# A two-layer selective scan: from states x channels on the partitions to directions x images x states

## The chip, the core and the metric

The kernel runs on one core of a Trainium2 chip. Its time is the device time of one execution in microseconds. The core has TensorE (PE), VectorE (DVE), ScalarE (ACT), GpSimd (POOL) and SyncE (SP), which here only issues DMAs; 16 DMA engines move data between DRAM and the on-chip memory SBUF. TensorE writes to PSUM, which GpSimd can't read.

## The reference

The input is 4 images of 64 x 64 pixels and 96 channels. Two layers of the same kind (L0, L1) are followed by two token layers (L2, L3; linear attention and a quantised feed-forward net). The change touches L0 and L1. Each of them computes, per image:

```
xn = group norm of x;  xx, z = in_proj(xn)          # 192 channels each
xc = silu(conv3x3_depthwise(xx) + b)
for k in 4 directions (rows, columns, both reversed), L = 4096 steps:
    dts, B, C = x_proj[k](xc in order k)              # 6, 16, 16
    delta = softplus(dt_proj[k](dts) + bias)          # 192 channels
    h[e, n] = exp(delta[e] * A[e, n]) * h[e, n] + delta[e] * u[e] * B[n]
    y_k[e]  = sum over 16 states n of h[e, n] * C[n]
y = y_0 + y_1 + y_2 + y_3 (put back in pixel order) + D * u
x = x + out_proj(layernorm(y) * silu(z))
```

The recurrence over 4096 steps runs for 2 layers x 4 images x 4 directions x 192 channels x 16 states. All of it is in 32-bit floats.

## The kernel before

Everything is written with tiles; a scheduler puts the instructions of each engine in order by the program's order and by what is ready, and sets the waits. Each engine then runs its instructions in that order.

`ssm_layer` does one layer, image by image: `conv(b)`, the scans, `finish(b)`. The convolution and the input projection are one set of nine matmuls per 512 pixels (L194). The 4096 steps are cut into 8 chunks of 512. A step of the loop is one direction k and one chunk c, 32 an image. For each, `chunk_inputs` makes B and C by matmuls whose weights repeat each state's row 8 times (L214), so that the partitions hold 16 states x 8 channels; delta by matmuls (L229) and a softplus from six instructions (L237 to L248); and du = delta * u (L253), which goes to a scratch in DRAM (L256).

The 192 channels make 6 groups of 32 per step, and each group 4 tiles of 128 partitions (16 states x 8 channels) x 512 steps. `load` (L274) reads du back with every row repeated 16 times, 1 MB a group. Per tile `scan` repeats delta over the states by a matmul from 32 partitions (L285, into PSUM), takes the exponential (L291), multiplies du by B on DVE (L293) and scans on DVE (L297, `tensor_tensor_scan`). `weigh` copies the carry (L304) and multiplies by C on POOL (L306). `sum` adds the 16 states with a matmul to 32 columns (L313), and `keep` adds the result to `y` (L337). The stages of a group are issued one to three groups behind its scan, and pieces of the next step's `chunk_inputs` after each group. The convolution and `finish` (z, layernorm, output projection; L352 to L385) stand alone before and after an image's scans.

A load's access pattern in DRAM is, with counts outermost first, 16 (states, step 0), 8 (channels), 2048 contiguous values; in SBUF it is 128 partitions of 2048 values.

Of the kernel before, what the change touches and what calls it, by code (L numbers as in the profile page):

```python
# [9 lines left out]
F32 = mybir.dt.float32  # L10
# [4 lines left out]
AX = mybir.AxisListType  # L15
# [3 lines left out]
B = 4  # L19
HW = 64  # L20
L = HW * HW
# [4 lines left out]
K = 4  # L26
PAD = HW + 2
# [3 lines left out]
EG = 8  # L31
NT = 4
NB = 3
NJ = NT * NB
P = 128
# [4 lines left out]
SQRT_HALF = 0.7071067811865476  # L40

# [15 lines left out]

def rows(t):

    if len(t.shape) == 2:  # L60
        return t.rearrange("p (r w) -> p r w", w=HW)
    return t.rearrange("p h (r w) -> p h r w", w=HW)


class Consts:
    def __init__(self, nc, pool, a):
        def load(name, shape):
            t = pool.tile(shape, F32, name=name)
            nc.sync.dma_start(t, a[name])
            return t  # L70

        self.rep = load("rep", [P, NB, 128])
        self.sel = load("sel", [128, NB, 32])
        self.group = load("group", [C, C])
        self.mask = load("mask", [C, C])
        self.mean_e = load("mean_e", [P, P])
        self.mean_c = pool.tile([C, C], F32, name="mean_c")
        nc.vector.memset(self.mean_c, 1.0 / C)
        self.eps = pool.tile([128, 1], F32, name="eps")
        nc.vector.memset(self.eps, EPS)  # L80
        self.one = pool.tile([128, 1], F32, name="one")
        nc.vector.memset(self.one, 1.0)


def neg_rsqrt(nc, cst, var, ln, r, sq, n=C):

    nc.scalar.activation(ln, var, AF.Ln, bias=cst.eps[:n])
# [6 lines left out]
@with_exitstack  # L94
def ssm_layer(ctx: ExitStack, tc, cst, a, pre, x_in, x_out):

    nc = tc.nc
    wp = ctx.enter_context(tc.tile_pool(name=pre + "w", bufs=1))
    big = ctx.enter_context(tc.tile_pool(name=pre + "big", bufs=1))
    cp = ctx.enter_context(tc.tile_pool(name=pre + "chunk", bufs=1))  # L100
    sp = ctx.enter_context(tc.tile_pool(name=pre + "scan", bufs=6))
    small = ctx.enter_context(tc.tile_pool(name=pre + "small", bufs=2))
    dp = ctx.enter_context(tc.tile_pool(name=pre + "dram", bufs=3, space=DRAM))
    p_da = ctx.enter_context(tc.tile_pool(name=pre + "p_da", bufs=4, space=PSUM))
    p_y = ctx.enter_context(tc.tile_pool(name=pre + "p_y", bufs=1, space=PSUM))
    p_b = ctx.enter_context(tc.tile_pool(name=pre + "p_b", bufs=2, space=PSUM))
    p_one = ctx.enter_context(tc.tile_pool(name=pre + "p_one", bufs=1, space=PSUM))


    in_w = wp.tile([C, 4 * P], F32, name="in_w")  # L110
    nc.sync.dma_start(in_w, a[pre + "in_proj_w"])
    taps = wp.tile([C, 9, 2 * P], F32, name="taps")
    nc.sync.dma_start(taps, a[pre + "conv_w"].unsqueeze(0).broadcast_to([C, 9, 2 * P]))

    def small_w(name, shape):
        t = wp.tile(shape, F32, name=name)
        nc.sync.dma_start(t, a[pre + name])
        return t

    conv_b = small_w("conv_b", [P, 2])  # L120
    dt_b = small_w("dt_projs_bias", [P, K, 2])
    ds_k = small_w("Ds", [P, 2, K])
    gam = small_w("gamma", [P, 2])
    bet = small_w("beta", [P, 2])
    out_w = small_w("out_proj_w", [P, 2, C])
    a_col = small_w("A_logs", [128, K, 2, NJ])
    xp_t = small_w("x_proj_t", [P, K, 2, R + 2 * NS])
    xp_dt = small_w("x_proj_dt", [R, K, 2 * P])
    dt_w = small_w("dt_projs_weight", [R, K, 2 * P])


    nc.vector.tensor_tensor(
        taps, taps, in_w[:, : 2 * P].unsqueeze(1).broadcast_to([C, 9, 2 * P]), ALU.mult
    )

    nc.scalar.activation(a_col, a_col, AF.Exp)
    nc.vector.tensor_scalar_mul(a_col, a_col, -1.0)
    ds = wp.tile([P, 2], F32, name="ds")
    nc.vector.tensor_reduce(ds, ds_k, AX.X, ALU.add)

    bc_w = wp.tile([P, K, 2, 2, 128], F32, name="bc_w")
    dl_w = wp.tile([P, K, 2, 2 * P], F32, name="dl_w")
    for k in range(K):
        for h in range(2):
            nc.vector.tensor_copy(
                bc_w[:, k, h].rearrange("p m (n e) -> p (m n) e", e=EG),
                xp_t[:, k, h, R:].unsqueeze(2).broadcast_to([P, 2 * NS, EG]),
            )
            ps = p_one.tile([128, TC], F32, name="ps1")
            nc.tensor.matmul(  # L150
                ps[:, : 2 * P], xp_dt[:, k, h * P : (h + 1) * P], dt_w[:, k, :], start=True, stop=True
            )
            nc.scalar.copy(dl_w[:, k, h], ps[:, : 2 * P])

    stats_of = {}

    def conv(b):

        xn = big.tile([C, PAD, PAD], F32, name="xn")
        nc.gpsimd.memset(xn[:, 0, :], 0.0)  # L160
        nc.gpsimd.memset(xn[:, PAD - 1, :], 0.0)
        nc.gpsimd.memset(xn[:, 1 : PAD - 1, 0], 0.0)
        nc.gpsimd.memset(xn[:, 1 : PAD - 1, PAD - 1], 0.0)
        st = small.tile([C, NC, 6], F32, name="st")
        for c in range(NC):
            mid = xn[:, 1 + ROWS * c : 1 + ROWS * (c + 1), 1 : 1 + HW]
            nc.sync.dma_start(mid, rows(x_in[b, :, c * TC : (c + 1) * TC]))
            nc.vector.bn_stats(st[:, c, :], mid)  # L168
        mv = small.tile([C, 2], F32, name="mv")
        nc.vector.bn_aggr(mv, st.rearrange("p c s -> p (c s)"))  # L170

        ps = p_one.tile([128, TC], F32, name="ps1")
        nc.tensor.matmul(ps[:C, :1], cst.group, mv[:, 0:1], start=True, stop=True)
        gs = small.tile([C, 2], F32, name="gs", bufs=3)
        nc.vector.tensor_copy(gs[:, 0:1], ps[:C, :1])
        d = small.tile([C, 1], F32, name="d")
        nc.vector.tensor_tensor(d, mv[:, 0:1], gs[:, 0:1], ALU.subtract)
        nc.vector.scalar_tensor_tensor(d, d, d, mv[:, 1:2], ALU.mult, ALU.add)
        ps = p_one.tile([128, TC], F32, name="ps1")
        nc.tensor.matmul(ps[:C, :1], cst.group, d, start=True, stop=True)  # L180
        ln = small.tile([C, 2], F32, name="ln")
        neg_rsqrt(nc, cst, ps[:C, :1], ln[:, 0:1], gs[:, 1:2], ln[:, 1:2])
        nc.vector.tensor_scalar_mul(gs[:, 1:2], gs[:, 1:2], -1.0)
        stats_of[b] = gs
        for c in range(NC):
            mid = xn[:, 1 + ROWS * c : 1 + ROWS * (c + 1), 1 : 1 + HW]
            nc.vector.tensor_scalar(mid, mid, gs[:, 0:1], gs[:, 1:2], ALU.subtract, ALU.mult)
        xc = big.tile([P, 2, L], F32, name="xc")
        for c in range(NC):
            for h in range(2):  # L190
                ps = p_one.tile([128, TC], F32, name="ps1")
                for tap in range(9):
                    dy, dx = divmod(tap, 3)
                    nc.tensor.matmul(  # L194
                        rows(ps),
                        taps[:, tap, h * P : (h + 1) * P],
                        xn[:, ROWS * c + dy : ROWS * (c + 1) + dy, dx : dx + HW],
                        start=tap == 0,
                        stop=tap == 8,
                    )  # L200
                nc.scalar.activation(  # L201
                    xc[:, h, c * TC : (c + 1) * TC], ps, AF.Silu, bias=conv_b[:, h : h + 1]
                )
        return xc

    def chunk_inputs(xc, k, c, got):


        u = scan_view(xc, k, c)
        got["b"] = p_b.tile([128, TC], F32, name="b_ps")  # L210
        c_ps = p_one.tile([128, TC], F32, name="ps1")
        for m, ps in enumerate((got["b"], c_ps)):
            for h in range(2):
                nc.tensor.matmul(rows(ps), bc_w[:, k, h, m], u[:, h], start=h == 0, stop=h == 1)  # L214
        yield
        got["c"] = cp.tile([128, TC], F32, name="cc", bufs=2)
        nc.scalar.copy(got["c"], c_ps)  # L217
        yield
# [3 lines left out]
        top = cp.tile([P, 2, TC], F32, name="t0")  # L222
        e = cp.tile([P, 2, TC], F32, name="t1")
        ln = cp.tile([P, 2, TC], F32, name="t2")
        w = cp.tile([P, 2, TC], F32, name="t3")
        for m in range(2):
            raw = p_one.tile([128, TC], F32, name="ps1")
            for h in range(2):
                nc.tensor.matmul(  # L229
                    rows(raw),  # L230
# [29 lines left out]
    class Group:  # L260

        def __init__(self, k, c, h, i, got, carry, xc, y):
# [390 lines left out]
```

## Time and profile before

| | |
|---|---|
| median of 3 runs | 17764.24 us (17760.72 to 17765.47) |
| profiled execution | 17765.74 us, of which 17763.9 us are the span |
| mean granted TensorE clock | 0.716 |
| matmuls, vector, scalar, GpSimd instructions | 34144, 15421, 12017, 6700 |
| DMA, main queue | 1765.94 MB, 353160 packets |
| one image's scans, from 195 to 1830 us | DVE 1518.68 us busy, PE 1437.60, POOL 1079.63, ACT 757.18 |

The span is the time between the first and the last instruction. A group's row in the profile has the line, the engine, output and inputs with their shapes, the count, the busy time of the group in us, the mean duration of one in ns, and the idle time of the engine before them with what ended it. Where several run at once, busy time is less than count times mean. A 32-bit matmul appears as two records, one for each of its two passes.

### The profile page before, as it was taken

What the parts mean: (1) busy time and instruction counts of PE and PEld (TensorE: products, weight loads), DVE (VectorE), ACT (ScalarE), POOL (GpSimd) and SP (SyncE); (2) the same over time, 40 slices, a digit from 0 to 9 for tenths busy, and PEclk for the clock granted to TensorE, in tenths of its full rate; (3) what the DMA queues carried; (4) which work ended last, traced back from release to release, by engine and by line L of the source; (5) the groups of instructions that cost most, each with busy time, mean ns of one, the idle gap of its engine ahead of it and who ended that gap; (6) DMA issues with size and microseconds to landing.
All of it is one profiled execution on the core that took longest, in us unless ns stands there. A gap on an engine that the chain in (4) does not pass through costs nothing.

```text
span 17763.9 us, 120237 instructions
## 1 busy us (share of the span) xinstructions
PE 14593.3 (82%) x34144; PEld 4171.9 (23%) x34144; DVE 13631.7 (77%) x15421; ACT 7698.0 (43%) x12017; POOL 8983.9 (51%) x6700
## 2 busy tenths in 40 slices
PE   8888788887888788887888788887888788885555
PEld 2222222222222222222222222222222222222222
DVE  5999399975999489984999579993999669993333
ACT  3444344443444344442444344442444334444555
POOL 3666166653666266652666356661666346660000
PEclk8767777667767777677776777677767777676665
DMA  4555165543555155542555255552555345550000
GB/s 88 129 128 128 40 133 129 128 98 74 129 128 129 41 126 129 128 106 62 133 124 131 60 109 127 130 122 48 131 128 129 71 96 128 129 126 23 7 7 7
DMA packets 360991, 1786.21 MB, mean 101 GB/s; under 512 B 93550, under 2 KB 94960, under 8 KB 162760
## 3 DMA queue, kind: packets, MB, share of 16 engines
q1 hardware_dynamic: 353160, 1765.94, 44.8%
q10 hardware_dynamic: 7168, 12.59, 0.2%
q8 instruction: 275, 4.51, 0.1%
q14 instruction: 388, 3.18, 0.1%
HBM read 1658.82 MB, written 119.54 MB: 100 GB/s over the span
## 4 chain that ended last, share of the span: by engine, by line
PE 41%; POOL 18%; DVE 17%; issue 15%; ACT 9%; DMA 0%; DVEq 0%; POOLq 0%; SPq 0%; ACTq 0%
POOL st L306 13%; PE da L285 11%; DVE st L297 9%; PE y_ps L313 8%; PE ps L194 6%; PE b_ps L214 5%; PE ps L229 4%; DVE st L293 3%; POOL delta L248 3%; POOL t L246 3%; ACT L88 1%; ACT da L291 1%; PE ps L362 1%; PE ps L370 1%; PE y_ps L383 1%
## 5 line engine op out<-in xcount | busy, mean ns | idle before, releaser
L306 POOL TENSOR_TENSOR st<-st,cc 128x512 f32<-128x512 f32 x6144 | 7785.6, 1298 | 4253.5 <-ACT carry L304 2489.1
L297 DVE TENSOR_TENSOR_SCAN st<-da,carry,st 128x512 f32<-128x512 f32 x5376 | 6460.2, 1264 | 662.8 <-ACT da L291 661.6
L285 PE MATMUL da<-delta,rep 32*128 32x512 f32 x12288 | 5498.9, 884 | 812.6 <-DVE st L297 723.7
L291 ACT ACTIVATE da<-da,A_logs 128x512 f32<-128x512 f32 x6144 | 3907.5, 664 | 4885.7 <-PE da L285 4876.1
L313 PE MATMUL y_ps<-st,sel 128*32 128x512 f32 x12288 | 3321.2, 913 | 798.5 <-POOL st L306 626.8
L293 DVE TENSOR_TENSOR st<-st,b_ps 128x512 f32<-128x512 f32 x6144 | 3788.2, 678 | 0.0
L285 PEld LDWEIGHTS da<-delta,rep 32*128 32x128 f32 x12288 | 1744.2, 245 | 4783.9 <-DVE st L297 3466.9
L229 PE MATMUL ps<-xc,dl_w 128*128 128x512 f32 x2048 | 1445.5, 834 | 23.5 <-ACT cc L217 12.6
L313 PEld LDWEIGHTS y_ps<-st,sel 128*32 128x32 f32 x12288 | 486.1, 137 | 3388.2 <-POOL st L306 1708.4
L246 POOL TENSOR_TENSOR t<-t,t 128x1024 f32<-128x1024 f32 x256 | 603.3, 2357 | 1047.5 <-DVE t L244 1047.5
L194 PE MATMUL ps<-xn,taps 96*128 96x512 f32 x2304 | 1047.4, 609 | 93.2 <-ACT xc L201 68.4
L214 PE MATMUL b_ps<-xc,bc_w 128*128 128x512 f32 x1024 | 980.8, 1052 | 73.5 <-DVE st L293 73.5
L253 DVE TENSOR_TENSOR du<-delta,xc 128x512 f32<-128x512 f32 x512 | 870.3, 1739 | 178.3 <-POOL delta L248 177.7
L237 ACT ACTIVATE t<-ps,dt_projs_bias 128x512 f32<-128x512 f32 x512 | 351.7, 687 | 1373.1 <-PE ps L229 1324.1
L297 DVE TENSOR_TENSOR_SCAN st<-da,st 128x512 f32<-128x512 f32 x768 | 876.2, 1201 | 50.5 <-ACT da L291 49.9
L214 PE MATMUL ps<-xc,bc_w 128*128 128x512 f32 x1024 | 874.4, 987 | 27.9 <-ACT t L238 21.7
L160 POOL MEMSET xn<- 96x66 f32 x8 | 1.2, 150 | 1762.7 <-PE ps L194 1598.0
L168 DVE BATCH_NORM_STATS2 st<-xn 96x6 f32<-96x512 f32 x64 | 44.2, 690 | 871.9 <-DMA xn<-x 437.2
L244 DVE SCALAR_TENSOR_TENSOR t<-t,t 128x1024 f32<-128x1024 f32 x256 | 329.3, 1286 | 426.0 <-ACT t L242 426.0
L484 POOL MEMSET tn<- 1x4096 f32 x8 | 28.0, 3506 | 1194.7 <-PE pa L525 1027.6
L229 PEld LDWEIGHTS ps<-xc,dl_w 128*128 128x128 f32 x2048 | 398.0, 205 | 949.8 <-issue 600.4
L248 POOL TENSOR_TENSOR delta<-t,t 128x1024 f32<-128x1024 f32 x256 | 600.7, 2347 | 3.1
(118 smaller groups left out, 8712.8 us busy)
## 6 DMA issues: line engine op xcount, KB each, us to landing
st<-scratch SPq DMA_DIRECT2D x1536, 1024.0 KB
scratch<-du SPq DMA_DIRECT2D x1024, 96.0 KB
xr<-in_x SPq DMA_DIRECT2D x64, 192.0 KB
x<-xr ACTq DMA_DIRECT2D x64, 192.0 KB
xr<-x SPq DMA_DIRECT2D x64, 192.0 KB
xn<-in_x SPq DMA_DIRECT2D x32, 192.0 KB
xn<-x SPq DMA_DIRECT2D x32, 192.0 KB
t<-x SPq DMA_DIRECT2D x4, 1536.0 KB
```

The lines of the kernel that those rows point to most:

```text
L194: nc.tensor.matmul(rows(ps), taps[:, tap, h * P : (h + 1) * P], xn[:, ROWS * c + dy : ROWS * (c + 1) + dy, dx : dx + HW], start=tap == 0, ...
L214: nc.tensor.matmul(rows(ps), bc_w[:, k, h, m], u[:, h], start=h == 0, stop=h == 1)
L229: nc.tensor.matmul(rows(raw), dl_w[:, k, h, m * P : (m + 1) * P], u[:, h], start=h == 0, stop=h == 1,)
L246: nc.gpsimd.tensor_tensor(ln, ln, w, ALU.subtract)
L248: nc.gpsimd.tensor_tensor(delta, top, ln, ALU.add)
L253: nc.vector.tensor_tensor(rows(du[:, h]), rows(delta[:, h]), u[:, h], ALU.mult)
L285: nc.tensor.matmul(da, cst.rep[part, i], self.got["delta"][part, h], start=True, stop=True)
L291: nc.scalar.activation(da, da, AF.Exp, scale=a_col[:, k, h, j : j + 1])
L293: nc.vector.tensor_tensor(st[:, t], st[:, t], self.got["b"], ALU.mult)
L297: nc.vector.tensor_tensor_scan(st[:, t], da, st[:, t], 0.0 if c == 0 else col, ALU.mult, ALU.add)
L306: nc.gpsimd.tensor_tensor(st[:, t], st[:, t], self.got["c"], ALU.mult)
L313: nc.tensor.matmul(y_of[h][32 * t : 32 * t + 32], cst.sel[:, i], self.st[:, t], start=i == 0, stop=i == NB - 1,)
```

## The change

Two images are processed together as a phase; there are four phases (two layers, two pairs). The partitions of a scan tile hold 8 (direction, image) pairs x 16 states, a tile is one channel x 512 steps, and a unit is 24 channels of one chunk: 256 units of 12 slots with two tiles each.

- `prepare` makes, for a whole phase, the convolution and then for each image, chunk and direction B, C, delta and du, and stores them in DRAM; softplus is one ACT function. It is written as a generator.
- `load` fetches du for a unit in six DMAs of 1 MB (four channels each), each row repeated over 16 partitions, and delta in twelve small ones. `times_b` multiplies du by B on POOL, 128 x 2048 at a time.
- `scan` is as before but for the matmul, which repeats delta from 8 partitions.
- `weights` builds per chunk, on POOL, matrices with C times a mask of the eight pairs. `contract` multiplies by C and sums over the states in one matmul per four time steps: 16 matmuls a call, to four column groups, moving operand 96 columns whose innermost step is 512 values. ACT copies the result and 16 DMAs a unit store it in DRAM in an order that keeps (pair, time).
- `finish` reads y from DRAM, adds the directions with permutation matmuls, and does layernorm with pixels on the partitions. It is a generator too.
- `run` issues scans slot by slot; after each slot 1.5 pieces of `finish` of the phase before and then of `prepare` of the next phase. The first `prepare` and the last `finish` stand alone. Pixels are stored in another order, so that the token layers' load is strided.

```diff
-    class Group:
...
+    def steps(self, ph, sp, xc, xp, dt_w, i, k, c):
...
+        for h in range(2):
+            nc.tensor.matmul(rows(ps[:XD]), xp[:, k, h], u[:, h], start=h == 0, stop=h == 1)
+        xd = sp.tile([XD, TC], F32, name="xd")
+        nc.scalar.activation(xd, ps[:XD], AF.Identity, bias=cst.one_row)
+        yield
+        nc.sync.dma_start(ph.bc[c][g], xd[: 2 * NS])
...
+        for m in range(2):
+            nc.scalar.activation(delta[:, m], raw[m][:C], AF.Softplus)
+        yield
+        nc.vector.tensor_tensor(rows(du), rows(delta), u, ALU.mult)
+        nc.sync.dma_start(ph.delta[c][g].rearrange("(h q) t -> q h t", h=2), delta)
+        yield
+        nc.sync.dma_start(ph.du[c][g].rearrange("(h q) t -> q h t", h=2), du)
...
+    def weights(self, ph):
...
+        for l1 in range(4):
+            cw = self.units.tile([128, 32, 4 * G], F32, name="cw", bufs=4)
+            for t in range(4):
+                b, m = divmod(t, 2)
+                self.nc.gpsimd.tensor_tensor(
+                    view(cw, t, (256, 4), (32, 8), (4, G)),
+                    view(ph.c_next, 256 * b + 64 * l1 + 8 * m, (16, 4), (1, 8), (0, G)),
+                    view(self.cst.gmask, 0, (0, 4), (0, 8), (1, G)),
+                    ALU.mult,
+                )
...
+    def load(self, u):
+        nc, ph = self.nc, u.ph
+        u.h = self.units.tile([128, EB, TC], F32, name="h")
+        u.dl = []
+        for s in range(EB // 8):
+            dl = self.units.tile([128, 2, TC], F32, name="dlt", bufs=2)
+            src = ph.delta[u.c].rearrange("g (i r) t -> r g i t", r=4)
+            first = (u.eb * EB + s * 8) // 4
+            for r in range(4):
+                nc.sync.dma_start(dl[32 * r : 32 * r + G], src[r, :, first : first + 2])
+            u.dl.append(dl)
+            for q in range(2):
+                e = s * 8 + q * 4
+                at = u.eb * EB + e
+                nc.sync.dma_start(
+                    u.h[:, e : e + 4].rearrange("p e t -> p (e t)"),
+                    ph.du[u.c][:, at : at + 4]
+                    .rearrange("g e t -> g (e t)")
+                    .unsqueeze(1)
+                    .broadcast_to([G, NS, 4 * TC]),
+                )
+    def times_b(self, u):
+        b = u.ph.b
+        for q in range(EB // 4):
+            h = u.h[:, 4 * q : 4 * q + 4]
+            self.nc.gpsimd.tensor_tensor(h, h, b.unsqueeze(1).broadcast_to([128, 4, TC]), ALU.mult)
+    def scan(self, u, n):
+        nc, ph = self.nc, u.ph
+        a = self.p_a.tile([128, 2, TC], F32, name="a")
+        for j in range(2):
+            e = 2 * n + j
+            part = slice(32 * (e % 4), 32 * (e % 4) + G)
+            nc.tensor.matmul(
+                a[:, j], self.cst.rep[part], u.dl[e // 8][part, (e % 8) // 4], start=True, stop=True
+            )
...
+    def contract(self, u, q):
+        nc, ph = self.nc, u.ph
+        l1, half = divmod(q, 2)
+        y = self.p_y.tile([128, TC], F32, name="y_ps")
+        for s in range(4):
+            l2 = half * 4 + s
+            for j in range(4):
+                nc.tensor.matmul(
+                    y[32 * j : 32 * j + 32, s * 4 * EB : (s + 1) * 4 * EB],
+                    u.cw[l1][:, 8 * j + l2],
+                    view(u.h, 64 * l1 + 16 * j + l2, (256, 2), (8, 2), (TC, EB)),
+                    start=True,
+                    stop=True,
+                )
...
+        for t in range(4):
+            b, m = divmod(t, 2)
+            dst = ph.y[:, u.c * 8 : u.c * 8 + 8, u.eb, 4 * b + l1].rearrange(
+                "g (j m) l e -> m j g (l e)", m=2
+            )[m]
+            nc.sync.dma_start(dst, u.d[t::4, t].rearrange("p l e -> p (l e)"))
...
+    def run(self, phases):
...
+        for at, u in enumerate(units):
+            for n in range(slots):
+                self.scan(u, n)
...
+                if at and n < 8:
+                    self.contract(units[at - 1], n)
...
+                if n == 8 and at + 1 < len(units):
...
+                    fetch(units[at + 1])
+                if n == 8 and at % per == 0:
+                    rest = behind(at // per)
+                    due = 0.0
+                due += rate
+                while due >= 1.0:
+                    next(rest, None)
+                    due -= 1.0
...
-        nc.sync.dma_start(t, x_in[b])
+        nc.sync.dma_start(t.rearrange("c (a p) -> c a p", p=64), x_in[b // 2, :, :, b % 2])
```

The pools `p_a`, `p_y` and `p_bg` (PSUM) and `units` have two buffers each, where a tile doesn't say otherwise. A layernorm slice in `finish` reads y of one (direction, image) pair with rows of 96 or 48 values:

```diff
+        for eh in range(2):
+            ys = []
+            for k in range(K):
...
+                t = fp.tile([128, n1, NEB // 2, n2 * EB], F32, name="yk", bufs=5)
+                for i in range(2):
+                    for l in range(n1):
+                        nc.sync.dma_start(
+                            t[64 * i : 64 * i + 64, l],
...
+                ys.append(t)
+                yield
+            for hi in range(2):
+                ps = self.bank()
+                for k, t in enumerate(ys):
...
+                    nc.tensor.matmul(
+                        ps[:, : 4 * C].rearrange("p (w b e) -> p w b e", w=4, b=NEB // 2),
+                        cst.perm[:, k],
...
```

## The prediction

> **What bounds the kernel now.** I read the page first: engine totals, the slices, the chain that ended last. Then the costliest groups (here with shapes kept apart), and then busy time by stage.
>
> ```profile
> span 17763.9 us, 120237 instructions
> PE 14593.3 (82%) x34144; PEld 4171.9 (23%) x34144; DVE 13631.7 (77%) x15421; ACT 7698.0 (43%) x12017; POOL 8983.9 (51%) x6700
> DVE  5999399975999489984999579993999669993333
> DMA  4555165543555155542555255552555345550000
> q1 hardware_dynamic: 353160, 1765.94, 44.8%
> PE 41%; POOL 18%; DVE 17%; issue 15%; ACT 9%; DMA 0%; DVEq 0%; POOLq 0%; SPq 0%; ACTq 0%
> ```
>
> No engine is full over the span, but the slices show eight plateaus (one per image and layer) with DVE at 9, a dip between them, and the token layers at the end. The DMA digit stays at 5 on the plateaus and no DMA is in the chain. The stages, by windows (columns: window, its length, PE, PEld, DVE, ACT, POOL busy, PE clock, DMA share, GB/s): the first convolution, the first image's scans, its layernorm, the token layers.
>
> ```profile
> 19.00:170.00 151.00, 137.40 (x306) 57.83 (x306) 8.40 (x21) 14.11 (x24) 0.00 (x0) 1.00 0.02 5
> 195.00:1830.00 1635.00, 1437.60 (x3454) 372.49 (x3450) 1518.68 (x1646) 757.18 (x1234) 1079.63 (x802) 0.70 0.58 129
> 1831.00:2036.00 205.00, 131.59 (x228) 40.74 (x220) 91.88 (x121) 74.38 (x89) 33.70 (x28) 0.68 0.16 39
> 16201.00:17763.00 1562.00, 829.68 (x2080) 364.45 (x2080) 593.39 (x998) 836.13 (x1152) 21.04 (x6) 0.63 0.03 8
> ```
>
> In the scans DVE is busy 1519 of 1635 us (93%) and PE 88%: DVE is the bound, PE close behind. Eight times 1635 is 13.1 ms; between the scans DVE idles eight times for about 0.36 ms.
>
> ```profile
> L306 POOL TENSOR_TENSOR st<-st,cc 128x512 f32<-128x512 f32 x6144 | 7785.6, 1298 | 4253.5 <-ACT carry L304 2489.1
> L297 DVE TENSOR_TENSOR_SCAN st<-da,carry,st 128x512 f32<-128x512 f32 x5376 | 6460.2, 1264 | 662.8 <-ACT da L291 661.6
> L285 PE MATMUL da<-delta,rep 32*128 32x512 f32 x12288 | 5498.9, 884 | 812.6 <-DVE st L297 723.7
> L313 PE MATMUL y_ps<-st,sel 128*32 128x512 f32 x12288 | 3321.2, 913 | 798.5 <-POOL st L306 626.8
> L293 DVE TENSOR_TENSOR st<-st,b_ps 128x512 f32<-128x512 f32 x6144 | 3788.2, 678 | 0.0
> L503 PE MATMUL vk_ps<-kv 128*96 128x96 f32 x512 | 82.5, 293 | 60.4 <-ACT kv L501 60.0
> ```
>
> **What the change does to the compute engines.** The number of scan tiles stays 6144 (4 phases x 8 chunks x 192 channels, each 128x512), so scans (7.3 ms), exponentials (3.9 ms, ACT) and rep matmuls (5.5 ms, PE) stay. DVE loses L293, 3.79 ms. POOL loses L306 (7.79 ms) and the softplus pieces L246/L248 (1.2 ms) and gains the B product: 1536 instructions of 128x2048, 4.7 us each (twice the 2.35 us of L246/L248 at 1024), 7.2 ms, plus 512 weight products of 256 elements at half an L306, 0.3 ms: 7.5 ms. For DVE remain 7.3 ms of scans, 0.87 ms of du (L253, 512 x 1.74 us, as slow as now because POOL still runs beside it) and about 0.8 ms of layernorm.
>
> PE swaps L313 for `contract`: 256 units x 128 = 32768 matmuls, two passes each, 65536 passes of 96 columns. L503 has that width: 82.5/512 = 0.161 us of busy time a pass. L313's passes go in fours to four column groups: 12288 x 0.913 = 11.2 ms of duration in 3.32 ms of busy time, 3.4-fold overlap. So `contract` costs 10.6 ms if nothing overlaps and 3.1 ms if it overlaps as L313; I take 3.1. Inputs: 1024 passes as L214 (0.91 to 0.96 us) and 1024 as L229 (0.71), 1.7 ms; convolution 1.05 ms as L194; layernorm about 1.0 ms (today's four groups sum to 0.85). PE sums to 12.4 ms, of which 11.4 lie in the overlapped middle; at today's 88% that is 13.0 ms. DVE's middle is 8.6 ms, POOL's 7.5.
>
> Ends that nothing covers: the first `prepare` two convolutions (0.30 ms) and 64 steps x 6.7 us of PE (0.43), 0.7 ms; the last `finish` two of today's (0.41 ms) plus 98304 y rows on 16 engines at 0.03 us (0.18), 0.6 ms; token layers 1.56 ms, their strided first load about as long as now. ACT gains 2048 copies of 128x384 (about 0.5 us, between L217 and L501), 1.0 ms, and loses most of the softplus chain; at some 7 ms it is covered. SP issues some 34 DMAs a unit of 24 tiles instead of 10; at 0.39 us (four writes took 1.55 us) that is 13 us a unit, covered.
>
> **The transfers.** This is the part that I think decides. The du broadcast keeps its size: 1536 loads of 1 MB in 8 KB rows. Its shape changes: today the source's outermost count is 16 (states), then 8 channels; afterwards it is 8 (direction x image), then 16 states. The destination has 128 partitions in both. Does the outer count set how many engines move a transfer? Three windows: loads with outer counts 16 and 128; du writes from 24 partitions alone; a weight load from 97 partitions alone.
>
> ```profile
> 1000.00:1010.00 10.00, 9.89 (x28) 3.11 (x24) 9.79 (x12) 9.54 (x15) 6.38 (x6) 0.84 0.99 212
> 196.30:198.40 2.10, 2.10 (x6) 0.97 (x4) 0.00 (x0) 2.09 (x4) 0.00 (x0) 0.61 0.74 185
> 16194.60:16195.20 0.60, 0.00 (x0) 0.00 (x0) 0.00 (x0) 0.00 (x0) 0.60 (x1) 0.50 0.07 23
> ```
>
> Shares are of 16 engines: 0.99 is all 16, 0.74 is 12, 0.07 is one. Twelve divides 24; nothing under 16 but 1 divides 97. So the split follows the outer count. Per engine that is 212/15.8 = 13.4, 185/11.8 = 15.6 and 23/1.1 = 21 GB/s (short rows, alone); the page gives 1765.94 MB / (0.448 x 16 x 17.76 ms) = 13.9. Sixteen loading engines are no slower each than twelve writing ones by more than 14%, so I read this as a limit of each engine, not of the memory. If the source's 8 governs, the load has 8 engines. The bounds: nothing lost (16 engines, or 8 at twice the rate) and half the rate. I take half: the row nearest in shape is the 24-partition one, and it says divisor.
>
> The Trainium skill ("DMA: Bandwidth & Descriptors", Rules for kernel authors) speaks against this change: it says that an outermost dimension of c < 16 on either side, a leading broadcast being its example, keeps the whole DMA on at most c engines. By that rule 8 engines are certain; by the rows here the destination's 128 could still give 16. The same page's line rate of about 27 GiB/s per engine would make 8 engines enough, and the kernel rival 1; the 13.4 of these loads speaks against it.
>
> Sum for the busiest engines in the middle: du 1610.6 MB / 8 / 13.4 GB/s = 15.0 ms. Delta, B and C rows: (100.7 + 16.8) MB / 8 engines, 2 KB rows at about 15 GB/s, 1.0 ms. The y stores have outer count 4: 131072 rows of 768 B over four engines at 0.036 us (the 97-partition rows, 768 B), 1.2 ms. Stores of delta and du, y reads and the rest, about 375 MB over 16 engines, three quarters in the middle: 1.2 ms. Together 18.4 ms, above PE's 13.0, which hides behind it.
>
> Waits that are added: `h` has two buffers, so loads of unit n+1 start when `contract` of unit n-1 is through, about 40 us into a 60 us load; that is early enough. The third `dlt` of a unit waits for the rep matmuls of the first, and behind it on SP queue two du loads and then the y stores; whoever waits is POOL's B product, then the scans. I price that at nothing while the rings are full, and up to 2 ms otherwise.
>
> **Forecast:** 0.7 + 18.4 + 0.6 + 1.56 = 21.26 ms, **21,300 us**, against 17763.9 of span (17765.7 for that execution, 1.8 us around it; the median is 17764.2, so no correction). Its own range is 18,700 (engines at 15.6 GB/s, smaller terms at their low ends) to 23,400 (2 ms of bubbles).
>
> **Rivals.**
> 1. *Faster: the loads keep their rate* (16 engines, or 8 at double). For: the destination has 128 partitions; the du loads' first rows could run faster from more distinct source rows. Against: the 24- and 97-partition windows. PE then bounds: 0.7 + 13.0 + 0.6 + 1.56 = 15.9 ms; 12.1 if `contract` and clock are ideal and DVE bounds (8.6/0.93). It decides from 140 GB/s on: there du takes 11.5 ms and the middle 14.9 ms, which with the ends is today's time.
> 2. *The strided reads of `contract` don't overlap.* Its moving operand steps 2 KB. L214 passes with 256 B steps take 0.86 us at full clock where others take 0.43, so strides cost; whether four groups share that is not shown. Unoverlapped: 11.4 + 7.5 = 18.9 ms of PE, /0.88 = 21.5, 24.3 ms in all.
> 3. *It doesn't do what it says: the pieces between the scans hold them up.* Every engine works in order, and a layernorm matmul behind a y load that sits behind 4 MB of du loads waits about 20 us: 3 phases x 16 waits x 20 us = 1.0 ms, convolution loads 0.5 ms. On rival 1 that gives 17.4 ms, about today's.
>
> **Chances.** Forecast 0.58, rival 1 0.27, rival 2 0.08, rival 3 0.07. All of rival 1 and half of rival 3 is faster by over 0.2% (about the least that a measurement of this kernel can tell from no change): 0.30; within 0.2%: 0.02; slower: 0.68. To hold the time 8 times in 10 the range must reach into rival 1: 14,500 to 23,400, leaving out rival 2, the ideal end of rival 1 and the tails.
>
> **What would show it.** Right: DMA share near 0.5 of 16 engines throughout the scans at 110 to 125 GB/s; h loads landing in about 10 us instead of 5; DVE at 4 to 5 tenths, its scans waiting for POOL's product and that for the DMA. Wrong: a DMA share of 0.8 or more or over 150 GB/s in the scans (rival 1); PE at 9 with `contract` over 40 us a unit (rival 2); PE waiting for y loads while the DMA is idle (rival 3).

## The result, and the profile after

The changed kernel takes 21005.96 us (median of 4 runs, 20987.32 to 21054.16) against 17764.86 us (17760.72 to 17766.56) for the kernel before on the same chip: a ratio of 1.1829, 95% interval 1.1809 to 1.185. It is 3.24 ms slower. The forecast was 21,300 us.

First the page of the changed kernel: span, engine totals, the slices of DVE and DMA, the main queue, the chain that ended last by engine.

```profile
span 20999.0 us, 224201 instructions
PE 14033.6 (67%) x88128; PEld 5993.9 (29%) x88128; DVE 8980.9 (43%) x8726; ACT 7346.5 (35%) x11582; POOL 7293.3 (35%) x2060
...
DVE  1233444444443444444443444444444444443333
...
DMA  2334444444443444444443444444444444444000
...
q1 hardware_dynamic: 1188612, 2270.66, 39.3%
...
ACT 4%; PE 4%; DVE 2%; DMA 1%; SPq 1%; POOL 0%; issue 0%; POOLq 0%; DVEq 0%; ACTq 0%
```

No compute engine is full any more, and no dip is left between the images: DVE stands at 4 nearly from end to end, where it stood at 9 on the plateaus. The DMA digit is 4 as well. The main queue moved 2270.66 MB, but its packets took 39.3% of 16 engines. The chain is little help here: its shares sum to 12%, so it reaches back only to the last units of the scans, at about 18.5 ms; the longest links there are du loads. The stages, by windows (columns as before: PE, PEld, DVE, ACT, POOL busy, PE clock, DMA share, GB/s): the first `prepare`, two stretches of scans with no pieces between them, and the token layers.

```profile
0.00:1000.00 1000.00, 770.74 (x1448) 218.29 (x1448) 190.51 (x184) 251.44 (x350) 66.58 (x32) 0.66 0.32 86
4000.00:4800.00 800.00, 504.79 (x4056) 220.36 (x4060) 384.12 (x320) 259.62 (x440) 365.66 (x95) 0.58 0.41 118
17000.00:17800.00 800.00, 498.12 (x3956) 215.88 (x3956) 377.39 (x314) 254.42 (x430) 370.79 (x111) 0.59 0.42 117
19450.00:21000.00 1550.00, 819.74 (x2161) 366.73 (x2159) 585.37 (x1006) 807.50 (x1122) 21.04 (x6) 0.65 0.04 8
```

In the scans the DMA share is 0.42 at 117 GB/s, where it was 0.58 at 129: less than 8 of 16 engines, and less data in a second. Counted over the trace's packets from 17000 to 17800 us, exactly eight are in flight for 62% of the time, and none of the 8 KB rows of du for 22%. The groups, with "idle before" and what ended it behind the second bar:

```profile
L342 POOL TENSOR_TENSOR h<-h,b 128x2048 f32<-128x2048 f32 x1536 | 6950.1, 4526 | 9779.9 <-DMA h<-du 8481.4
L351 PE MATMUL a<-dlt,rep 8*128 8x512 f32 x12288 | 6576.0, 1041 | 4840.5 <-DVE h L360 4772.0
L360 DVE TENSOR_TENSOR_SCAN h<-a,carry,h 128x512 f32<-128x512 f32 x5376 | 6487.7, 1265 | 7383.0 <-POOL h L342 5135.9
...
L383 PE MATMUL y_ps<-h,cw 128*32 128x96 f32 x65536 | 3144.7, 347 | 760.1 <-issue 292.2
```

Follow the last column from PE: the rep matmul waits for the scan (4772.0 us), the scan for POOL's product (5135.9), and the product for the du load (8481.4). These waits end in L330's loads. What do the loads wait for? SP issues them, so its own waits tell (columns: us in all, times, longest):

```profile
SPq L404 <- DMA h<-du: 3500.6, 721, 9.0
SPq L325 <- PE a L351: 3432.9, 273, 82.9
```

The y stores (L404) go out when a du load lands, though they read nothing of it; I take that for want of room in the queue, which no run shows by itself. The delta loads (L325) wait for the rep matmuls that read the `dlt` tile before. One unit of the last phase, with no pieces beside it, shows how it plays out (start, length, instruction):

```profile
17408.23 7.15 SPq L404 DMA_DIRECT2D y<-d  x8
...
17416.76 1.28 SPq L330 DMA_DIRECT2D h<-du  x2
...
17428.60 4.60 POOL L342 TENSOR_TENSOR h<-h,b 128x2048 f32<-128x2048 f32 x1 [18.45 <-DMA h<-du]
...
17437.45 4.49 POOL L342 TENSOR_TENSOR h<-h,b 128x2048 f32<-128x2048 f32 x1 [4.25 <-DMA h<-du]
...
17447.70 28.55 SPq L404 DMA_DIRECT2D y<-d  x8
```

The next unit's first load is issued only after the y stores have left, its first product starts 12 us later, and POOL has stood for 18.45 us. From then on products follow every 9 to 10 us, as the loads land. Meanwhile the next eight y stores take 28.55 us to get through SP's queue. Over the thirteen units of the window, the packets show 48.0 us a unit in which du rows flow and 13.5 us in which none does. From the last du row of a unit to the issue of the next unit's first du load it is 12.1 us, and 10.0 of them pass at the y stores: 4.6 in issuing them, 5.4 in waiting, mostly for ACT's copies.

### The profile page after: what moved, and what is told of

Same layout as the page of the kernel before. It is cut to its first block, busy times and chain, and to the rows that moved or that the text cites. A ratio compares the mean times of both kernels' runs of the same rounds, so it can differ in the third digit from the quotient of the medians.

```text
span 20999.0 us, 224201 instructions
## 1 busy us (share of the span) xinstructions
PE 14033.6 (67%) x88128; PEld 5993.9 (29%) x88128; DVE 8980.9 (43%) x8726; ACT 7346.5 (35%) x11582; POOL 7293.3 (35%) x2060
## 3 DMA queue, kind: packets, MB, share of 16 engines
q1 hardware_dynamic: 1188612, 2270.66, 39.3%
## 5 line engine op out<-in xcount | busy, mean ns | idle before, releaser
L342 POOL TENSOR_TENSOR h<-h,b 128x2048 f32<-128x2048 f32 x1536 | 6950.1, 4526 | 9779.9 <-DMA h<-du 8481.4
L351 PE MATMUL a<-dlt,rep 8*128 8x512 f32 x12288 | 6576.0, 1041 | 4840.5 <-DVE h L360 4772.0
L360 DVE TENSOR_TENSOR_SCAN h<-a,carry,h 128x512 f32<-128x512 f32 x5376 | 6487.7, 1265 | 7383.0 <-POOL h L342 5135.9
L356 ACT ACTIVATE a<-a,a_col 128x512 f32<-128x512 f32 x6144 | 4048.0, 662 | 7313.1 <-PE a L351 7214.1
L351 PEld LDWEIGHTS a<-dlt,rep 8*128 8x128 f32 x12288 | 1635.0, 285 | 8575.5 <-DVE h L360 8101.2
L383 PE MATMUL y_ps<-h,cw 128*32 128x96 f32 x65536 | 3144.7, 347 | 760.1 <-issue 292.2
L383 PEld LDWEIGHTS y_ps<-h,cw 128*32 128x32 f32 x65536 | 2550.7, 142 | 2520.1 <-issue 2143.9
L392 ACT COPY d<-y_ps 128x384 f32<-128x384 f32 x2048 | 954.6, 482 | 2214.6 <-PE y_ps L383 1584.4
L360 DVE TENSOR_TENSOR_SCAN h<-a,h 128x512 f32<-128x512 f32 x768 | 886.4, 1206 | 1095.2 <-POOL h L342 726.3
L222 PE MATMUL bg<-xn,taps 96*96 96x512 f32 x2304 | 1022.7, 606 | 51.8 <-DVE xn L208 51.8
L303 POOL TENSOR_TENSOR cw<-c,gmask 128x256 f32<-128x256 f32 x512 | 320.9, 685 | 1966.8 <-PE y_ps L383 1252.7
```

Source lines behind the costliest of these rows:

```text
L222: nc.tensor.matmul(rows(ps[:C]), taps[:, tap, h * C : (h + 1) * C], xn[:, ROWS * c + dy : ROWS * (c + 1) + dy, dx : dx + HW], start=tap == ...
L303: self.nc.gpsimd.tensor_tensor(view(cw, t, (256, 4), (32, 8), (4, G)), view(ph.c_next, 256 * b + 64 * l1 + 8 * m, (16, 4), (1, 8), (0, G)) ...
L342: self.nc.gpsimd.tensor_tensor(h, h, b.unsqueeze(1).broadcast_to([128, 4, TC]), ALU.mult)
L351: nc.tensor.matmul(a[:, j], self.cst.rep[part], u.dl[e // 8][part, (e % 8) // 4], start=True, stop=True)
L356: nc.scalar.activation(a[:, j], a[:, j], AF.Exp, scale=ph.a_col[:, at : at + 1])
L360: nc.vector.tensor_tensor_scan(u.h[:, e], a[:, j], u.h[:, e], 0.0 if u.c == 0 else ph.carry[:, at : at + 1], ALU.mult, ALU.add,)
```

## The experiments

The theory: the source's outermost count of 8 puts the du loads on 8 engines, and that makes the loss (16 engines would bring the old time back or better). The rival, from the gap of 13.5 us: the loop of stores, loads and buffers costs as much as the engines do. Times are compared with the kernel before on the same chip. Unit times are counted from the first POOL product of a unit to that of the next, "quiet" where no pieces of other phases are issued, "busy" in the first 31 units of the middle phases.

**The states outermost.** The partitions hold states x pairs instead of pairs x states, so that the loads of du, B and C have an outermost count of 16; `rep`, the mask and the A columns follow.

```diff
-                    .unsqueeze(1)
-                    .broadcast_to([G, NS, 4 * TC]),
+                    .unsqueeze(0)
+                    .broadcast_to([NS, G, 4 * TC]),
```

> The changed kernel, but the partitions are ordered states x pairs instead of pairs x states, so the source of the du, B and C loads has outer counts 16 (states), 8 (pairs); bytes, rows and every other instruction stay. Theory (the outer count of 8 puts these loads on 8 engines, and that bounds the scans): 16 engines move them, about 210 GB/s while they run, a 1 MB load in about 5 us; PE becomes the bound as in rival 1, near 15,900 us (14,500 to 17,500). Rival (the two h buffers, SP's order and the pieces between the scans leave the gaps, and the number of engines is not it): over 20,000 us.

Measured: 19237.65 us, ratio 1.0827 (1.0809 to 1.0845). The windows answer (a quiet stretch, columns as above), and SP's waits:

```profile
16000.00:17000.00 1000.00, 700.43 (x5738) 308.33 (x5730) 546.79 (x454) 368.55 (x622) 542.40 (x162) 0.60 0.66 137
```
```profile
SPq L325 <- PE a L351: 4017.2, 263, 101.4
SPq L404 <- DMA h<-du: 1857.4, 560, 5.3
SPq L404 <- ACT d L392: 1563.1, 402, 9.6
```

The DMA share rises from 0.42 to 0.66: more than eight engines, so the count governs. That gives back 1.77 of the 3.24 ms; the time lies between the two expectations. But a quiet unit falls only from about 60 us to 52.2: its rows flow for 34 us instead of 48, and the stretch with none grows from 13.5 to 18.5 us. The theory holds for the split, and it is only half of the loss.

**The kernel before with its loads on 8.** The converse: the old kernel's partitions turned to 8 channels x 16 states; the constants follow, and the loops stay as they are.

```diff
-                src[self.h, self.i].unsqueeze(0).broadcast_to([NS, EG, NT * TC]),
+                src[self.h, self.i].unsqueeze(1).broadcast_to([EG, NS, NT * TC]),
```

> The kernel before, with its partitions ordered channels x states, so that its du loads have outer counts 8, 16 instead of 16, 8. Theory: 8 engines move them. A step of six loads and four writes then takes 6 x 9.8 + 2.3 = 61 us at the 13.4 GB/s per engine of the prediction and 6 x 7.4 + 2.3 = 47 us at the 17.6 GB/s (8192 B in 0.466 us) that the changed kernel's loads show, against 51 us that DVE needs: about 20,300 us by the first rate, 17,800 to 18,300 by the second; DMA share at most 0.5 to 0.6 in the scans. Rival (the 128 partitions of the destination decide): 17,764 us within 0.3%, DMA share as before.

Measured: 18557.68 us, ratio 1.0456 (1.0426 to 1.0486). The first image's scans, and the chain that ended last:

```profile
195.00:1830.00 1635.00, 1420.88 (x3234) 373.14 (x3238) 1424.29 (x1543) 704.53 (x1146) 1017.55 (x754) 0.69 0.48 120
```
```profile
PE 29%; DMA 28%; DVE 14%; ACT 10%; POOL 10%; issue 9%; SPq 0%; DVEq 0%; POOLq 0%; ACTq 0%
```

Share 0.48 instead of 0.58, and DMA, which had 0% of the chain, has 28%. The time lies between the two expectations, nearer to that of the faster rate: 120 GB/s over 0.48 of 16 engines is 15.6 GB/s an engine, more than the 13.4 on which the sum was built. This loop, which has six buffers for its loads, loses 0.8 ms by the split alone.

**The loads by themselves.** 64 loads of 1 MB for each of four access patterns: outermost 16 repeats x 8 rows; 8 rows x 16 repeats, the rows close together; the same 393 KB apart; 128 different rows.

> Loads alone, none of the reference's work (the output is a copy of x): 64 loads of 1 MB in 8 KB rows in each of four forms: outer 16 with step 0 then 8 rows; outer 8 rows then 16 with step 0; the same with rows 393 KB apart; 128 distinct rows. Theory: first and last form on 16 engines at 205 to 225 GB/s, the two middle ones on 8 engines (share 0.5) at 107 GB/s if an engine is limited to 13.4, at 141 if to 17.6. Rival (one common limit of about 215 GB/s): the middle forms also reach 200 GB/s.

Measured, by SP's timeline with one line per pattern (it tells when SP issued the loads, which runs ahead of the transfers: the packets of the four patterns span 307, 594, 584 and 193 us), and by two lines of the page:

```profile
0.73 271.01 SPq L29 DMA_DIRECT2D h<-in_x  x64
275.98 572.97 SPq L32 DMA_DIRECT2D h<-in_x  x64
849.00 594.50 SPq L35 DMA_DIRECT2D h<-in_x  x64
1443.54 207.67 SPq L38 DMA_DIRECT2D h<-in_x  x64
```
```profile
DMA  9999999555555555555555555555555555999998
GB/s 209 219 219 219 219 219 219 129 112 114 114 114 113 114 113 113 113 112 114 113 113 113 113 113 113 113 113 114 113 113 113 113 113 120 154 369 423 418 321 248
```

The split without anything else around it: 219 GB/s on 16 engines, 113 on half of them, at either distance of the rows; 13.7 and 14.1 GB/s an engine. The Trainium skill's rule that was weighed in the prediction ("DMA: Bandwidth & Descriptors", Rules for kernel authors), at most as many engines as the outermost count, holds here.

**Fewer pieces a slot.** `rate = 0.75` instead of 1.5, so that pieces of other phases spread over the whole phase.

> The changed kernel with 0.75 instead of 1.5 pieces of prepare and finish after each slot, so that they spread over a whole phase. Theory (transfers bound, in both halves of a phase): the same bytes in the same engines, 20,600 to 21,100 us. Rival 3 (pieces hold the scans up through the order of the queues, 85 us units against 60): up to 1.1 ms less, about 19,900 us.

Measured: 20423.39 us, ratio 1.1499 (1.1459 to 1.1539), 0.58 ms less than the change and between the two expectations. Busy units fall from 88 us to 74, while the later units rise from 60 to 68. Pieces lengthen the units that they stand beside, and less so where they are thin. The packets say how: in the busy units of the change du rows flow for 48.3 us, hardly more than in the quiet ones (46.8 us over all phases), but none flows for 40.7 us instead of 13.7. In these gaps (5400 to 7600 us) the 16 engines have a share of 0.32, and for 40% of the time no packet at all is in flight: the next loads are held back.

**The contraction and the next loads earlier.** Two calls of `contract` a slot in slots 0 to 3, the next loads at slot 4 instead of 8. First on the change, then on the version with the states outermost.

```diff
-                if at and n < 8:
-                    self.contract(units[at - 1], n)
+                if at and n < 4:
+                    self.contract(units[at - 1], 2 * n)
+                    self.contract(units[at - 1], 2 * n + 1)
```

> The changed kernel with its eight contract calls two to a slot in slots 0 to 3, and the next unit's loads issued at slot 4 instead of 8; nothing else moves. Loop theory (the second h buffer comes free too late, so that every unit has a gap of 10 to 20 us in which POOL waits for the first load): the gap closes, but with 8 engines six loads need 45 to 58 us, so a quiet unit goes from 60 to 50-57 us and the time to 19,000-20,200 us. Engine theory alone (8 engines are full): no more than 1%, 20,800 us or more.

> Both: states outermost (16 engines) and contract in slots 0 to 3 with the loads at slot 4. Loop theory: with the load at 5 us and the gap closed a quiet unit comes down from 52 us to PE's 37-42 us, in all 16,500 to 17,500 us, faster than the kernel before. Rival (what is left is neither buffer nor engines, but the pieces between the scans and the order of the queues): within 3% of 19,238 us.

Measured: 21334.96 us, 1.2004 (1.1984 to 1.2024), and 19243.51 us, 1.0829 (1.0812 to 1.0845): slower by 0.33 ms, and nothing (quiet unit still 52.2 us). The place in the program doesn't hold the loads; they wait for something in the loop.

**A third dlt.** `bufs=3` for `dlt`, on the version with the states outermost (the convolution's input tile has one buffer to make room).

> States outermost, and three dlt buffers instead of two (the input rows of prepare have one buffer instead of two, to make room), so that no dlt load waits for a rep matmul of its own or the next unit. If the wait of the third dlt, which the prediction priced at nothing to 2 ms and which SP shows as 4.0 ms of waiting, delays the du loads behind it: 1 ms or more under 19,238 us. If the h buffer and the y stores are what comes last: within 1%.

Measured: 19319.09 us, 1.0878 (1.0861 to 1.0894); quiet unit 52.2 us. So the largest of SP's waits there, the delta loads for the rep matmuls, is not what delays the unit: the wait just moves elsewhere.

**The y stores off SP's queue, or a third d.** On the version with the states outermost, either the stores are issued from ACT's queue or the tile that they empty has three buffers (and the convolution's input tile one instead of two, to make room).

```diff
-            nc.sync.dma_start(dst, u.d[t::4, t].rearrange("p l e -> p (l e)"))
+            nc.scalar.dma_start(dst, u.d[t::4, t].rearrange("p l e -> p (l e)"))
```
```diff
-            u.d = self.units.tile([128, 4, 8, EB], F32, name="d")
+            u.d = self.units.tile([128, 4, 8, EB], F32, name="d", bufs=3)
```

> With loads on 16 engines (19238 us) a unit still takes 52 us between the pieces and 75 to 84 us beside them. Theory A: the y stores stand on SP's queue behind du loads that wait for a free h buffer, contract waits for a d buffer that those stores have yet to empty, and the h buffer waits for contract: a circle with a bubble of some 10 us a unit. Issued from ACT's queue instead, the stores are out of it: quiet unit 42 to 47 us, 17,900 to 18,500 us in all. Theory B: the bubble comes from h having two buffers of 24 tiles and contract running late for its own reasons (PE's order); then the time stays at 19,100 to 19,300, or rises a little, because ACT's exponentials now stand behind stores that wait for a copy.

> As the states-outermost version, with a third d buffer and y stores left on SP (the convolution's input tile has one buffer instead of two). Theory A: contract's later calls no longer wait for the stores of two calls before; quiet unit 45 to 49 us, 18,300 to 18,900 us. Theory B: d isn't what contract waits for: 19,150 to 19,350 us.

Measured: 18202.06 us, 1.0246 (1.023 to 1.0261), and 19086.43 us, 1.0745 (1.0729 to 1.0761). A quiet stretch of the first, and SP's waits over its whole span:

```profile
14900.00:15900.00 1000.00, 732.69 (x6690) 342.80 (x6688) 637.02 (x530) 425.00 (x728) 628.95 (x181) 0.60 0.70 159
```
```profile
SPq L325 <- DMA y<-d: 3211.5, 880, 15.9
SPq L325 <- PE a L351: 2162.7, 315, 121.7
```

Moving 16 stores a unit to another queue gains 1.04 ms: quiet units fall from 52.2 to 45.1 us, to 159 GB/s. The stretch of 18.5 us without du rows shrinks to one of 5.7 us a unit, with three short ones beside it, 14.5 us in all, and the loads start early enough for the scans to go on. All of the gain lies in the quiet units: the busy ones take 85.4 us, where they took 83.9. The circle of theory A is there: with the states outermost the last matmul of `contract` ended on average 12.0 us after a unit's last du row, and with the stores on ACT's queue it ends 12.4 us before it (quiet units). But the link that counts is the place of the stores in SP's queue. With the third d `contract` too ends early, 15.5 us before the last du row, and still the next load is issued only 13.5 us after it, 1.8 us behind the last y store; so the third d gains only 0.15 ms, and the time lies just below theory B's range. With the stores on ACT's queue SP's delta loads wait mostly for y stores in flight (3211.5 us), so the stores still hold the loads up, only less.

**All together.** The states outermost, early contraction, third dlt and `rate = 0.75`; then the same with the y stores on ACT's queue; then that with a third d in place of the third dlt.

> States outermost, contract in slots 0 to 3, three dlt buffers, 0.75 pieces a slot. If the terms add: 16,000 to 16,800 us, PE near 85% in the scans; if the pieces and the waits overlap each other, like e6 within 2%.

> The combination (states outermost, contract in slots 0 to 3, third dlt, 0.75 pieces a slot; 18377 us) with the y stores on ACT's queue. Theory A: another 0.6 to 1.2 ms, 17,200 to 17,800 us, about even with or below the kernel before. Theory B: 18,250 to 18,500 us.

> The combination with y stores on ACT's queue, and a third d in place of the third dlt. Theory A with d as its main link: 17,000 to 17,700 us, below the run with the third dlt. Theory B: 18,300 to 18,700 us, since nothing that comes last is changed.

Measured: 18376.56 us, 1.0344 (1.0329 to 1.036); 18380.66 us, 1.0349 (1.0333 to 1.0364); 18441.87 us, 1.038 (1.0362 to 1.0397). The gains don't add: the first lies between its two expectations, the other two where theory B put them. With the pieces spread over the phase, units beside them take 62 to 69 us wherever the y stores are issued; in the last phase's later units, which have none beside them, the stores on ACT's queue do help (52.3 to 47.2 us). What bounds the units with pieces, once the split and the stores are mended, stays open; the trace of the version with the stores on ACT's queue hints at the other DMAs in SP's queue. In its busy units `contract` is through and the y stores are out 3 us after the last du row, but the next du load is issued only 47 us after it, behind delta loads that wait for rep matmuls and the pieces' own loads and stores, which wait for what the pieces compute. No run moved those to another queue. No version beat the kernel before; the best is 0.44 ms above it.

## Why the prediction was right, and where its terms were off

**Right: the split.** The du loads run on as many engines as the source's outermost count, 8 of them, and the scans wait for POOL, POOL for the loads. All three signs that were named came: a share of 0.41 to 0.42 (expected near 0.5) at 117 GB/s (110 to 125); a load every 9 to 10 us; DVE at 4, its scans waiting for POOL's product and that for the load. Taking the split out of the new kernel and putting it into the old one moves the time in the expected direction: -1.77 ms and +0.8 ms.

**The size of the middle is right, its terms are not.** Middle and ends, predicted and measured (phase starts from the trace; the middle runs from 0.81 ms to about 19.04):

| term | predicted | measured |
|---|---|---|
| first `prepare` | 0.7 ms | 0.81 ms |
| du loads on 8 engines | 15.0 ms, 58.6 us a unit | 48.0 us a unit, x 256 = 12.3 ms |
| rows of delta, B, C and y, and waits | 2.2 ms, waits nothing to 2 ms | 13.5 us a unit without du rows, 3.4 ms |
| everything else beside the scans | 1.2 ms | 2.7 ms |
| last `finish` | 0.6 ms | 0.41 ms |
| token layers | 1.56 ms | 1.55 ms |

The fourth row is counted from the units with pieces beside them: 31 units a phase, longer than that phase's quiet ones by 20, 28, 27 and 10 us, 85 us in all, x 31. The measured column gives 21.2 ms, 0.2 above the span, because the window's units are 0.8 us longer than the mean quiet unit (x 256 = 0.2 ms).

*The du term is 2.7 ms too large.* The step that failed is the rate of 13.4 GB/s per engine, taken from a window in which 16 engines ran without a pause. With eight loading, 6.29 MB in 48.0 us is 16.4 GB/s an engine. The packets are shorter: 0.47 us on average in the quiet window, falling from 0.56 at the start of a unit's stretch to 0.40 at its end, against 0.64 in the version on 16 engines. But loads alone, without pause, stayed at 14.1 (0.59 us a packet). Why eight engines go faster in the kernel than by themselves was not tried and stays open.

*The row with the waits is 1.2 ms too small, and that of the pieces 1.5 ms.* "I price that at nothing while the rings are full" was the failing sentence: they are not full, since the unit's y stores stand in SP's queue ahead of the next loads, and no du row moves for 13.5 us a unit. So SP's issuing, 13 us a unit, was not "covered". Nor was the other row right in kind. It priced the pieces' bytes on the busy engines; in fact, of the 28 us by which the pieces lengthen a unit in the middle phases, 27 are time without du rows. That is rival 3's mechanism, pieces that hold the scans up, inside the forecast's own case; how much of that time the pieces' transfers need and how much is waiting, no run separates. The errors cancel: that the total came within 0.3 ms is luck, from one term too large and two too small.

**Rival 1 was wrong twice.** Its condition fails, as said. But where its condition is given, 16 engines and 137 GB/s, the kernel still takes 19.24 ms and not 15.9; the waits and pieces that the forecast under-priced were left out of the rival altogether. No run bears out its 0.27 of chance for "faster": even with 159 GB/s, above the 140 from which it was to decide, the time is 18.20 ms.

**Rival 2 is refuted.** `contract` was put at 3.1 ms, if its four column groups overlap as L313's did; it took 3144.7 us. The ACT copies (predicted 1.0 ms, measured 954.6 us) and POOL's weights (0.3 ms, 320.9 us) hold too. PE's total was under-priced: 13.2 ms without the token layers (14.0 less 0.8) instead of 12.4. The rep matmul, as wide as before but over 8 partitions instead of 32, went from 884 to 1041 ns a pass, 1.1 ms in all; the granted clock fell from 0.70 in the old scans to 0.59 in the quiet ones of the new kernel, by about the same factor. The loads hide it.

## What to carry to other kernels

Before changing what the partitions hold, write down the outermost count of every load and store that it changes, and count the engines: a load of the same bytes in the same rows had half of them. Then look at what shares a queue with the critical loads: 16 small stores a unit in front of them cost 1 ms here, more than a buffer could win back. A total that comes out right is no proof of its terms; the test is to remove each one by itself.

## What the runs showed of the hardware

The same 1 MB in 8 KB rows to 128 partitions took 3.0 us a load from 128 different rows, against 4.8 us when eight rows were read sixteen times each, both on 16 engines (64 loads in 193 and 307 us by their packets; page slices of up to 423 against 219 GB/s; 0.35 against 0.60 us a packet on average). The 13.4 GB/s an engine, read in the prediction as a limit of each engine, is thus a limit of these repeated reads: with other rows the same engines go 1.6 times as fast on average and about twice as fast at the peak. Which part of the path sets it, no run here shows.
